# A chunked gated delta rule inside an eight-layer kernel: a feed-forward block is spread over another part of its work, and the second half's channels move beside the chunk recurrence

## The chip, the cores and the metric

The kernel runs on one core of a Trainium2 chip. The metric is device time in microseconds (us), from launch to end, as the median of several runs. One further execution was recorded by the hardware profiler, and all readings of single instructions come from it.

## The reference

The input is a batch of 1 x 1024 tokens of width 256. Eight blocks follow each other, each with a layer norm in front and a residual sum behind: `attn_a`, `ffn`, `attn_b`, `ffn` (the same weights as the first), `attn_c`, `moe`, `attn_d`, `moe`. The change touches the second to the fourth block only:

```python
# ffn: ternary weights, wq = clip(round(W / mean|W|), -1, 1) * mean|W|
hidden = silu(x @ wu.T) * (x @ wg.T)          # 256 -> 1024
y = hidden @ wd.T                             # 1024 -> 256

# attn_b: q, k (6 heads x 32) and v (6 heads x 64) pass a causal convolution of
# 4 taps and a silu, q and k are normalized, then token by token, per head:
S = S * exp(g_t)                              # S is 32 x 64
delta = (v_t - k_t @ S) * beta_t
S = S + outer(k_t, delta)
o_t = q_t @ S
# o is normalized per head, multiplied by silu(gate), and projected to 256
```

## The kernel before

The tokens are held as 8 tiles (chunks) of 128, in two halves of 512 (`HALF`). The function `middle` computes the second to the fourth block. The recurrence is not run token by token: within a chunk of 128 tokens it becomes matrix products with the inverse of a triangular matrix per head, and a state is carried from chunk to chunk.

Work is written as Python generators; each `yield` ends a step. `weave(main, side)` draws steps of `main` and, after each, on average `pace` steps of `side`; `at(rate, steps)` sets the pace while its steps are drawn. `one_by_one` runs generators after each other, `in_turn` alternates them, `staggered` starts one every few steps, and `times(3, ...)` yields only at every third step. The order in which steps are drawn is the order in which instructions are recorded; the framework then arranges each engine's instructions by its own estimate, and on the chip each engine runs its list strictly in order.

These generators matter:

- `ffn_steps(hf, ...)` (L597): the feed-forward block for one half. For each of 8 slices `e` of the 1024 hidden units it issues 6 bf16 matmuls for `f_wu` (tile `pf`), a silu on ScalarE, 6 bf16 matmuls for `f_wg`, a product on VectorE (`sl`), and `split`, which cuts the fp32 result into three bf16 pieces `hT` with ScalarE and GpSimd. Three slices later `second(e)` issues 12 matmuls into the two PSUM tiles `po`, which `sums()` takes. A last step adds `po` to the residual `x` (L647). There are 25 steps.
- `channels(hf, cv)` (L1131): the layer norm of a half (if not yet made), then for 6 groups `j` of 128 channels a projection (`pj`), a copy into `raw` (ScalarE), a convolution of one multiplication and three multiply-adds on VectorE (L797, L800), a silu, and transposes to tokens (`pt`, L817); for `q` and `k` also sums of squares (`pn`). In between come the projections for `g` and `beta` (`pg`).
- `products(hf, p)` (L1159): `decays` (`g`, and its exponentials through `pe`) and, per chunk, `prepare` (L849): GpSimd makes `kA`, `gm` and `qA`; TensorE multiplies `gm` and adds the causal mask (`pd`, L867 and L869), ScalarE takes the exponential, TensorE transposes (`pt`, L878) and multiplies (`pk`, L888), VectorE writes `am` (L892), and SyncE sends 4 pieces of it to DRAM (`dA`).
- `invert(hf, p)` (L903): one load of the 96 triangular blocks of 32 x 32 of a half (4 chunks), 31 elimination steps of two VectorE instructions each (L916, L922), and two stores. `relay` (L929) loads the results into `xi` and `xiT`.
- `turns(p)` (L1171): per chunk `complete` (first matmul `py`, L964), and the `chain` of the state, which runs one chunk behind. `leave` (L1067) normalizes a chunk's output, projects it (`pw`) and adds it to `x`.

The order in `middle` is written out by hand: the first half of the second block's feed-forward (L697); `channels(0)` with the second half of that feed-forward beside it at a pace of 0.75 (L1210); then one weave whose main line is `products(0)`, `invert(0)`, and then `relay`, `turns` and `leave` alternating, and whose side line is `second_half()` (L1229): `channels(1)` at 1.0, `products(1)` at 1.2, then `invert(1)` and `ahead`, which makes the fourth block's norm and the first half of its feed-forward once the first four chunks have left. The second half of that feed-forward comes last (L1248).

The PSUM pool of `middle` has five banks that all the small tiles share, and the two `po` tiles. The causal mask is added by a matmul of two fp32 operands, the mask and three copies of the identity:

```python
id3 = sq[:, IDENT : IDENT + 1, :].to_broadcast([P, GRP, P])
pe.matmul(pd, lhsT=sq[:, GT, :], rhs=gm[:, h0 : h0 + GRP, :], start=True, stop=False)
pe.matmul(pd, lhsT=sq[:, CAUSAL, :], rhs=id3, start=False, stop=True)
```

Of the kernel before, what the change touches and what calls it, by code (L numbers as in the profile page):

```python
# [15 lines left out]
BF16 = mybir.dt.bfloat16  # L16
# [6 lines left out]
P = 128  # L23
# [9 lines left out]
FF = 1024  # L33
# [4 lines left out]
IDENT, LE, GT, CAUSAL = range(4)  # L38
# [3 lines left out]
def hybrid_kernel(ctx: ExitStack, tc: tile.TileContext, w: dict, out: bass.AP):  # L42
# [554 lines left out]
    def ffn_steps(hf, wt, xT, p, bank, sums, beside=None):  # L597

        cols = slice(hf * HALF, (hf + 1) * HALF)
        po = sums()
        hT = {}

        def second(e):
            h = hT.pop(e)
            for t in range(HT):
                for n in range(3):
                    pe.matmul(  # L610
                        po[t // 2][:, t % 2, :],
                        lhsT=h[:, n, t * P : (t + 1) * P],
                        rhs=wt["f_wd"][:, e, :],
                        start=(e == 0 and t % 2 == 0 and n == 0),
                        stop=(e == FF // P - 1 and t % 2 == 1 and n == 2),
                    )

        for e in range(FF // P + 3):
            if e < FF // P:
                both = []  # L620
                for wn in ("f_wu", "f_wg"):
                    ps = bank("pf")
                    mm(
                        ps,
                        [
                            (wt[wn][:, k, e * P : (e + 1) * P], xT[:, n, k, cols])
                            for k in range(KC)
                            for n in range(3)
                        ],
                    )  # L630
                    if wn == "f_wu":
                        sl = p.tile([P, HALF], F32, tag="sl", name="sl")
                        act.activation(sl, ps, AF.Silu, scale=wt["f_sc"][:, 0, 0:1])  # L633
                        yield
                    else:
                        dve.tensor_tensor(sl, sl, ps, ALU.mult)  # L636
                hT[e] = p.tile([P, 3, HALF], BF16, tag="hT", name="hT", bufs=4)
                split(p, hT[e], sl, [HALF], pool)
                if beside:
                    beside()  # L640
                yield
            if e >= 3:
                second(e - 3)
                yield
        for t in range(HT):
            i = hf * HT + t
            dve.scalar_tensor_tensor(x[:, i, :], po[t // 2][:, t % 2, :], wt["f_both"], x[:, i, :], ALU.mult, ALU.add)  # L647
        yield


    def middle(wf, wt, n_f, norm, weights, following):
# [25 lines left out]
        with (  # L677
# [16 lines left out]

            f2 = right.enter_context(tc.tile_pool(name="f2", bufs=2, side="right", reuse_waits="tile"))
            n_f.need(0, bank)
            for _ in ffn_steps(0, wf, n_f.xT, f2, bank, sums, lambda: n_f.step(1, bank)):  # L697
                pass

            xT = norm.xT  # L700
            qk = b1.tile([P, NT, 2 * DH, DK], F32, tag="qk", name="qk")
# [13 lines left out]
            eT = b1.tile([ROWS, NT, 2], F32, tag="eT", name="eT")  # L715
            le6 = sq[:, LE : LE + 1, :].to_broadcast([P, DH, P])
            past = b1.tile([P, 6, 3], F32, tag="past", name="past")
            id3 = sq[:, IDENT : IDENT + 1, :].to_broadcast([P, GRP, P])

            def decays(hf, gb, p):  # L720

# [127 lines left out]
            def prepare(c, p):  # L849

                while c >= HOLD and c - HOLD not in done:
                    yield
                kA = two_of(pool, p, "kA", c, 0)
                gm = p.tile([P, DH, P], F32, tag="gm", name="gm")
                pool.tensor_tensor(gm, le6, g[:, c, :, None].to_broadcast([P, DH, P]), ALU.mult)
                qA = p.tile([P, 2, DH, DK], F32, tag="qA", name="qA")
                pool.tensor_tensor(
                    qA,
                    qk[:, c, None, :DH, :].to_broadcast([P, 2, DH, DK]),
                    cq[:, c, :, :, None].to_broadcast([P, 2, DH, DK]),  # L860
                    ALU.mult,
                )
                yield
                dT = p.tile([P, DH, P], F32, tag="dT", name="dT", bufs=2)
                for h0 in range(0, DH, GRP):
                    pd = bank("pd")[:, : GRP * P].rearrange("p (h n) -> p h n", h=GRP)
                    pe.matmul(pd, lhsT=sq[:, GT, :], rhs=gm[:, h0 : h0 + GRP, :], start=True, stop=False)  # L867

                    pe.matmul(pd, lhsT=sq[:, CAUSAL, :], rhs=id3, start=False, stop=True)  # L869
                    act.activation(dT[:, h0 : h0 + GRP, :], pd, AF.Exp)  # L870
                yield
                kqT = p.tile([ROWS, 2, 3, P], F32, tag="kqT", name="kqT")
                qGT[c] = hold.tile([ROWS, 2, P], F32, tag="qGT", name="qGT")
                for n in range(2):
                    hs = slice(n * GRP, (n + 1) * GRP)
                    pt = bank("pt")[:ROWS].rearrange("p (i n) -> p i n", i=4)
                    for i, src in enumerate((kA[:, 0, hs], kA[:, 1, hs], qA[:, 0, hs], qA[:, 1, hs])):
                        pe.transpose(pt[:, i, :], src.rearrange("p h d -> p (h d)"), ident)  # L878
                    act.copy(kqT[:, n], pt[:, :3, :])
                    act.copy(qGT[c][:, n], pt[:, 3, :])  # L880
                yield
                am[c] = hold.tile([P, DH, 2, P], F32, tag="am", name="am")
                for n in range(2):
                    made = []
                    for i in range(GRP):
                        r = slice(i * DK, (i + 1) * DK)
                        pk = bank("pk")[:, : 2 * P].rearrange("p (i n) -> p i n", i=2)
                        pe.matmul(pk, lhsT=kqT[r, n, 0, :], rhs=kqT[r, n, 1:, :], start=True, stop=True)  # L888
                        made.append(pk)
                    for i, pk in enumerate(made):  # L890
                        h = n * GRP + i
                        dve.tensor_tensor(  # L892
                            am[c][:, h], pk, dT[:, h : h + 1, :].to_broadcast([P, 2, P]), ALU.mult
                        )
                    yield
                for b in range(NB):
                    r = slice(b * BL, (b + 1) * BL)
                    nc.sync.dma_start(out=blocks(dA, c, b), in_=am[c][r, :, 0, r])
                yield
# [202 lines left out]
            def in_turn(*steps):  # L1102

                steps = list(steps)
                while steps:
                    steps = [s for s in steps if next(s, steps) is not steps]
                    yield

            def one_by_one(*steps):
                for s in steps:  # L1110
                    yield from s
# [47 lines left out]
            def products(hf, p):  # L1159

                yield from decays(hf, steps_of.pop(hf), p)
                lengths(hf, lens.pop(hf))
                cs = range(hf * HC, (hf + 1) * HC)
                for c in cs:
                    pool.tensor_tensor(
                        vb[:, c], vb[:, c], beta[:, c, :, None].to_broadcast([P, DH, DV]), ALU.mult
                    )
                yield
                yield from staggered(2, [prepare(c, p) for c in cs])
# [13 lines left out]
            def at(rate, steps):  # L1183

                pace[0] = rate
                yield from steps

            def weave(main, side):

                debt = 0.0  # L1190
                for _ in main:
                    debt += pace[0]
                    while debt >= 1.0:
                        next(side, None)
                        debt -= 1.0
# [11 lines left out]
            for pair in still:  # L1207
                for t in pair:
                    pool.memset(t, 0.0)
            side = at(0.75, ffn_steps(1, wf, n_f.xT, f2, bank, sums))  # L1210
            next(side)
            weave(channels(0, cv), side)
            for _ in side:
                pass
            right.close()
# [11 lines left out]
                yield from ffn_steps(0, wf, n_g.xT, f3[0], bank, sums)  # L1227

            def second_half():  # L1229
                yield from at(1.0, channels(1, cv))  # L1230
                yield from at(1.2, products(1, p2))
                fronts.close()
                yield from at(1.2, in_turn(one_by_one(times(3, invert(1, b3)), relay(1, 8)), ahead()))

            side = second_half()
            next(side)
            leaving = staggered(5, [leave(c, bt) for c in range(NT)])
            weave(
                one_by_one(
                    products(0, p2), times(3, invert(0, b3)), in_turn(relay(0, 6), turns(bt), leaving)  # L1240
                ),
                side,
            )
            for _ in in_turn(side, (n_g.step(1, bank) for _ in range(HT + 2))):
                pass
            right.close()
# [364 lines left out]
```

## Time and profile before

| | |
|---|---|
| time, median of 5 runs | 1779.19 us (1777.99 to 1783.81) |
| the profiled execution's own time | 1781.2 us |
| its span, first to last instruction | 1779.1 us |
| its mean granted TensorE clock | 0.940 |
| TensorE matmuls (PE) busy | 1612.2 us, 91% |
| VectorE (DVE) busy | 924.3 us, 52% |
| ScalarE (ACT) busy | 617.9 us, 35% |
| GpSimd (POOL) busy | 381.4 us, 21% |
| the part of `middle` that is rearranged | from 354.9 to 764.1 us of the span |

In the lines of the profile, PE is TensorE's matmuls, DVE VectorE, ACT ScalarE, POOL GpSimd and SP SyncE, which issues the DMAs. L12 is line 12 of the kernel. A line of the timeline gives the start, the time taken by one or several instructions that were merged, the instruction, and in brackets the idle time before it and what ended that. A table of windows gives for each stretch of the span the busy time of each engine, with the number of instructions, and the TensorE clock that was granted (1.00 is full speed). A full-rate matmul of 128 x 512 bf16 elements takes about 0.22 us when it follows another.

### The profile page before, as it was taken

The numbers are of one execution on the slowest core, as the hardware profiler recorded it, in microseconds if no ns is written. First come the engines' busy times: TensorE is split into PE (matmuls) and PEld (weight loads), VectorE is DVE, ScalarE is ACT, GpSimd is POOL, SyncE is SP. The second block draws the span as 40 slices with busy tenths as digits, with TensorE's granted clock in tenths as the row PEclk, the third lists the DMA queues.
The fourth block names the chain that finished last, engine by engine and source line by source line (L and its number), as shares of the span: only waits on it lengthen the run. The fifth ranks groups of instructions, "written<-read, shape, count | busy, mean of one in ns | idle before, by whom it ended". The sixth has DMA issues, their size and how long they took to land.

```text
span 1779.1 us, 23924 instructions
## 1 busy us (share of the span) xinstructions
PE 1612.2 (91%) x9655; PEld 747.6 (42%) x9674; DVE 924.3 (52%) x1762; ACT 617.9 (35%) x1117; POOL 381.4 (21%) x474
## 2 busy tenths in 40 slices
PE   7999999987749598789999998999889999998999
PEld 2433433544437366434333334454333333444454
DVE  7767675466736734357777634134554444533211
ACT  1466567445513131314554551111022222231100
POOL 2000002634213232440000000533101111230433
PEclk9999999997959698789999998999999999996999
DMA  5000000000010100120000001000000000000000
GB/s 185 1 1 1 1 2 1 1 1 0 18 34 19 25 10 1 45 99 1 1 1 1 2 1 55 1 1 0 0 1 1 1 1 1 1 1 1 1 12 12
DMA packets 33549, 24.23 MB, mean 14 GB/s; under 512 B 21888, under 2 KB 29776, under 8 KB 33440
## 3 DMA queue, kind: packets, MB, share of 16 engines
q1 hardware_dynamic: 32432, 18.89, 3.7%
q0 software_dynamic: 1008, 3.83, 0.6%
q8 instruction: 76, 1.25, 0.3%
q14 instruction: 33, 0.27, 0.0%
HBM read 19.10 MB, written 3.41 MB: 13 GB/s over the span
## 4 chain that ended last, share of the span: by engine, by line
PE 75%; DVE 15%; POOL 5%; issue 2%; ACT 2%; DMA 1%; SPq 0%; POOLq 0%; DVEq 0%; ACTq 0%
PE s L258 19%; PE st L258 9%; PE o L270 8%; PE po L160 5%; PE pj L160 4%; DVE mx L218 3%; PE py L1385 2%; PE pu L1370 2%; PE pu L1285 2%; PE pg L1285 2%; PE pg L1370 2%; PE pf L160 2%; PE stt L258 2%; POOL hT L101 1%; POOL rest L99 1%
## 5 line engine op out<-in xcount | busy, mean ns | idle before, releaser
L218 DVE TENSOR_REDUCE mx<-s 128x2 f32<-128x1024 f32 (+3 forms) x352 | 401.4, 1150 | 177.5 <-PE st L258 138.2
L258 PE MATMUL st<-qT,kT 32*128 32x512 f32 (+3 forms) x1288 | 390.1, 614 | 1.7 <-ACT pr L245 0.9
L258 PE MATMUL s<-kT,qT 32*128 32x512 f32 (+3 forms) x1408 | 358.0, 612 | 13.5 <-DVE mx L218 10.9
L243 ACT ACTIVATE pr<-st 128x512 f32<-128x512 f32 (+3 forms) x408 | 205.2, 553 | 266.7 <-PE st L258 211.1
L270 PE MATMUL o<-pr,V 128*32 128x256 f32 (+3 forms) x2240 | 200.2, 429 | 0.5
L245 ACT ACTIVATE pr<-st,bonus 128x512 f32<-128x512 f32 x236 | 149.5, 684 | 70.5 <-PE st L258 70.0
L258 PEld LDWEIGHTS s<-kT,qT 32*128 32x128 f32 x1408 | 102.6, 183 | 163.0 <-issue 133.1
L258 PEld LDWEIGHTS st<-qT,kT 32*128 32x128 f32 x1288 | 129.6, 183 | 17.6 <-ACT pr L243 6.5
L270 PEld LDWEIGHTS o<-pr,V 128*32 128x32 f32 x2240 | 45.4, 108 | 205.3 <-issue 188.2
L316 POOL TENSOR_TENSOR raw<-raw,rc 128x512 f32<-128x512 f32 x24 | 25.1, 1048 | 484.1 <-DVE rc L315 484.1
L1374 DVE TENSOR_TENSOR sl<-sl,pg 128x512 f32<-128x512 f32 (+1 forms) x48 | 32.9, 686 | 137.3 <-PE pg L1370 137.3
L258 PE MATMUL s<-kr,qr 64*128 64x512 f32 (+3 forms) x384 | 89.9, 542 | 11.0 <-DVE mx L218 7.6
L1375 POOL TENSOR_TENSOR hT<-sl,mask 128x512 f32<-128x512 f32 (+1 forms) x48 | 60.6, 1264 | 176.7 <-DVE sl L1374 176.7
L1372 ACT ACTIVATE sl<-pu 128x512 f32<-128x512 f32 (+1 forms) x48 | 28.6, 596 | 195.9 <-PE pu L1370 195.9
L258 PE MATMUL st<-qr,kr 64*128 64x512 f32 (+3 forms) x344 | 78.8, 501 | 0.0
L249 POOL TENSOR_SCALAR_AFFINE_SELECT pr<-pr 128x128 f32<-128x128 f32 x128 | 35.7, 294 | 181.0 <-ACT pr L243 179.7
L215 DVE TENSOR_TENSOR s<-s,squares 128x256 f32<-128x256 f32 x64 | 27.5, 429 | 78.2 <-PE s L258 73.6
L258 PEld LDWEIGHTS s<-kr,qr 64*128 64x128 f32 x384 | 30.3, 187 | 72.1 <-issue 21.3
L160 PE MATMUL pf<-xT,f_wu 128*128 128x512 bf16 x182 | 50.8, 403 | 3.3 <-ACT xT L100 1.6
L610 PE MATMUL po<-f_wd,hT 128*128 128x256 bf16 x384 | 48.4, 277 | 5.6 <-POOL hT L101 3.0
L1370 PE MATMUL pu<-z,m_up_B 128*128 128x512 f32 (+1 forms) x96 | 49.6, 599 | 0.0
L636 DVE TENSOR_TENSOR sl<-sl,pf 128x512 f32<-128x512 f32 x32 | 21.9, 686 | 53.1 <-ACT sl L633 30.0
(352 smaller groups left out, 2360.3 us busy)
## 6 DMA issues: line engine op xcount, KB each, us to landing
qT<-nmT SPq DMA_DIRECT2D x96, 2.0 KB
x<-in_x SPq DMA_DIRECT2D x8, 128.0 KB
raw_f_wu<-in_f_wu SPq DMA_DIRECT2D x1, 1024.0 KB
raw_f_wg<-in_f_wg SPq DMA_DIRECT2D x1, 1024.0 KB
raw_f_wd<-in_f_wd SPq DMA_DIRECT2D x1, 1024.0 KB
out<-x SPq DMA_DIRECT2D x8, 128.0 KB
b_wqkv<-in_b_wqkv SPq DMA_DIRECT2D x1, 768.0 KB
dA<-am SPq DMA_DIRECT2D x32, 24.0 KB
```

Of the source, the lines that this page charges most:

```text
L160: pe.matmul(ps, lhsT=a, rhs=b, start=(n == 0), stop=(n == len(pairs) - 1))
L218: dve.reduce_max(maxima[u][:, pair : pair + 2, t % HT, c // HALF], ps[:, :, :size], axis=AX.X, negate=True)
L243: act.activation(pr[:, js, :wide], ps, AF.Exp)
L245: act.activation(pr[:, js, :wide], ps, AF.Exp, bias=bias[:, kt : kt + 1])
L249: pool.affine_select(block, block, [[1, P]], ALU.is_ge, 0.0, base=0, channel_multiplier=-1)
L258: pe.matmul(dst, lhsT=a, rhs=b, start=(i == 0), stop=(i == len(parts) - 1))
L270: pe.matmul(sums[u][32 * j : 32 * j + 32, c0:c1], lhsT=V[:, kt, g * GH + j, :], rhs=weights[m][0][:, j, c0 - d : c1 - d], start=(kt == 0 a ...
L610: pe.matmul(po[t // 2][:, t % 2, :], lhsT=h[:, n, t * P : (t + 1) * P], rhs=wt["f_wd"][:, e, :], start=(e == 0 and t % 2 == 0 and n == 0), ...
L1285: pe.matmul(ps[:r], lhsT=wt[wn][:, k, es], rhs=xT[:, k, cols], start=(k == 0), stop=False)
L1370: pe.matmul(ps[:r], lhsT=wt[wn][:, es], rhs=z[hf, m, j], start=False, stop=True, skip_group_check=(j > 0))
L1375: pool.tensor_tensor(hT[:r], sl[:r], masks[3 + j][:r, cols], ALU.mult)
L1385: pe.matmul(ld[hf][j], lhsT=wt["m_down_A"][:r, e, :], rhs=tops_of[n, j][:r], start=(e == 0), stop=(e == HIDC - 1),)
```

## The change

Four edits, all in `middle` and in `ffn_steps`:

1. `sums()` is called when the first `second(e)` runs rather than at the start of the generator. The first half's feed-forward is run for 21 of its 25 steps only; its last four (three groups of 12 `po` matmuls, and the sum into `x`) are then drawn alternately with the first four steps of the second half's, and three more of these follow.
2. The rest of the second half's feed-forward is side work at a pace of 0.4 beside a main line of `channels(0)`, `products(0)`, `invert(0)` and `relay(0)`; what is left of it is drawn after that.
3. `channels(1)`, `products(1)`, `invert(1)` and `ahead` are side work beside `turns` and `leave` alone, at paces of 2.4 and, from `invert(1)` on, 1.0.
4. The identity and the causal mask are copied to bf16 tiles by GpSimd (two instructions in all), and the mask's matmul takes these.

```diff
-        po = sums()
-        hT = {}
+        po, hT = [], {}
         def second(e):
+            if e == 0:
+                po.extend(sums())
...
-            for _ in ffn_steps(0, wf, n_f.xT, f2, bank, sums, lambda: n_f.step(1, bank)):
-                pass
+            opening = ffn_steps(0, wf, n_f.xT, f2, bank, sums, lambda: n_f.step(1, bank))
+            for _ in range(2 * (FF // P) + 5):
+                next(opening)
...
-            id3 = sq[:, IDENT : IDENT + 1, :].to_broadcast([P, GRP, P])
+            ident16, causal16 = (b1.tile([P, P], BF16, tag=n, name=n) for n in ("ident16", "causal16"))
+            pool.tensor_copy(ident16, ident)
+            pool.tensor_copy(causal16, sq[:, CAUSAL, :])
+            id3 = ident16[:, None, :].to_broadcast([P, GRP, P])
...
-                    pe.matmul(pd, lhsT=sq[:, CAUSAL, :], rhs=id3, start=False, stop=True)
+                    pe.matmul(pd, lhsT=causal16, rhs=id3, start=False, stop=True)
...
-            side = at(0.75, ffn_steps(1, wf, n_f.xT, f2, bank, sums))
-            next(side)
-            weave(channels(0, cv), side)
+            side = at(0.4, ffn_steps(1, wf, n_f.xT, f2, bank, sums))
+            for _ in opening:
+                next(side)
+            for _ in range(3):
+                next(side)
+            weave(one_by_one(channels(0, cv), products(0, p2), times(3, invert(0, b3)), relay(0, 6)), side)
...
             def second_half():
-                yield from at(1.0, channels(1, cv))
-                yield from at(1.2, products(1, p2))
+                yield from at(2.4, channels(1, cv))
+                yield from products(1, p2)
                 fronts.close()
-                yield from at(1.2, in_turn(one_by_one(times(3, invert(1, b3)), relay(1, 8)), ahead()))
+                yield from at(1.0, in_turn(one_by_one(times(3, invert(1, b3)), relay(1, 8)), ahead()))
             side = second_half()
-            next(side)
             leaving = staggered(5, [leave(c, bt) for c in range(NT)])
-            weave(
-                one_by_one(
-                    products(0, p2), times(3, invert(0, b3)), in_turn(relay(0, 6), turns(bt), leaving)
-                ),
-                side,
-            )
+            weave(in_turn(turns(bt), leaving), side)
```

## The prediction

> **What bounds the kernel now.** I read the totals and slices of the page first, then busy time by windows over the rearranged part (354.9 to 764.1 us), then the PE timeline around its gaps.
>
> ```profile
> span 1779.1 us, 23924 instructions
> PE   7999999987749598789999998999889999998999
> PEclk9999999997959698789999998999999999996999
> ```
>
> PE is the limit nearly everywhere; the slices that fall to 4 and 5 lie in `middle`, and the clock falls with them. The windows show how much (columns: PE, PEld, DVE, ACT, POOL busy, granted clock):
>
> ```profile
> 369.00:413.00 44.00, 42.94 (x250) 27.32 (x252) 30.89 (x56) 26.20 (x45) 19.67 (x27) 1.00 0.00 1
> 413.00:421.20 8.20, 0.00 (x0) 0.00 (x0) 8.03 (x36) 3.58 (x5) 4.67 (x5) 0.72 0.00 0
> 431.30:463.40 32.10, 29.58 (x142) 17.02 (x140) 17.60 (x37) 19.80 (x38) 10.97 (x12) 0.89 0.06 10
> 480.10:509.60 29.50, 0.00 (x0) 0.03 (x1) 22.89 (x57) 2.86 (x4) 9.72 (x10) 0.58 0.10 29
> 509.60:528.40 18.80, 15.32 (x114) 12.20 (x115) 1.97 (x7) 3.90 (x9) 1.80 (x2) 0.50 0.22 34
> 528.40:568.20 39.80, 38.73 (x377) 28.59 (x375) 23.09 (x67) 15.61 (x37) 14.64 (x16) 0.99 0.05 9
> 594.00:623.60 29.60, 13.38 (x32) 6.42 (x33) 21.51 (x76) 6.39 (x12) 5.59 (x7) 0.62 0.17 39
> ```
>
> Where PE has a filler (369 to 413, 528 to 568) it is over 97% busy at full clock. It stands still for 8 us while the norm follows the feed-forward, for 29.5 us in the first inversion, and for half of 594 to 623.6 in the second. After a stop the clock stays at 0.50 for 18.8 us. The timeline names each stop's end:
>
> ```profile
> 360.60 0.69 PE L140 MATMUL u<-squares,xn 128*128 128x128 f32 x2 [4.38 <-DVE xn L137]
> 421.29 1.08 PE L140 MATMUL u<-squares,xn 128*128 128x128 f32 x4 [8.33 <-DVE xn L137]
> 431.36 0.81 PE L867 MATMUL pd<-gm,squares 128*128 128x384 f32 x2
> 432.01 0.81 PE L869 MATMUL pd<-squares 128*128 128x384 f32 x2
> 509.60 1.36 PE L964 MATMUL py<-xi,am 32*32 32x32 f32 x24 [29.59 <-DMA xi<-dX]
> 623.67 1.30 PE L964 MATMUL py<-xi,am 32*32 32x32 f32 x24
> ```
>
> Three moments carry the sum: first `pd` 431.4, first `py` 509.6 (turn 0), fifth `py` 623.7 (turn 4).
>
> **What the built order says.** In the changed kernel's PE list all 96 `pf` and 95 of the 96 `po` matmuls of the spread half stand before the first `pd`: at pace 0.4 beside some 34 channel steps, with seven drawn ahead, 20 of 25 steps are gone, and the framework puts the rest ahead of the products too. So nothing of the feed-forward fills inversion 0; PE only has two `pg` matmuls near its end. The work that did lie beside `products(0)`, `channels(1)`, is now among turns 0 to 3. `products(1)` ends inside turn 3 instead of before it. Before turn 4 the list has 48 `pf` and 20 `po` of the fourth block's feed-forward; in the trace 11 `pf` came before it. SP's DMAs keep their order. The two GpSimd copies (0.3 us each, half a 128x256 `rest` of 0.65) stand far ahead, where POOL idles; without that cover they cost 0.6. The later `sums()` costs nothing: `po` is free once L647 has read it, and its first matmul stands behind the norm's transposes.
>
> **Step 1, carried-over opening.** PE has five `pf` groups (1.3 us each: six matmuls 0.216 us apart) to do while DVE makes the norm, so the 4.38 us gap goes, and the half-clock rows behind it (2.77 and 2.13 us for six `pf` that take 1.46). PE work from 354.9 to 413: 9.04 + 42.94, less 2.6 for two groups done earlier, less 2 of half clock, plus 1 of waits = 48.4; it ends at 403. The gap of 8.3 goes too: the norm of half 1 no longer stands ahead of `products(0)`.
>
> **Step 2, to the first `pd`.** Behind the last `pf` (399.5) the chain is `sl` 0.69, cast 0.60, table load 1.28, Ln 0.22, nine small DVE operations 2.5, `gm` 1.47 and semaphores: 8 to 9 us. POOL has `rest`, `hT` and four `vb` (3.2) ahead of `gm` and is ready at about the same time. First `pd` at 408, 23 earlier; 4 us of PE wait are in it.
>
> **Step 3, `products(0)` alone.** Each chunk on PE: two `gm` matmuls 0.65, two masks, eight `pt` 0.87, six `pk` 1.28. The mask in fp32 shows two records and 0.65 us; in bf16 no row shows 384 columns, `pf` with 512 takes 0.216, so 0.16, bounded by 0.16 and 0.65. That is 0.48 x 16 = 7.7 us of PE over both halves, half on the path. 3.8 us per chunk plus waits on ACT and the five banks: 4.5 to 5, where the trace has 5.4 with PE full. Four chunks and a tail of 4.5: last `am` at 432 against 463.5.
>
> **Step 4, inversion 0.** From last `am` to first elimination 9.2 us (463.5 to 472.7), unchanged. The elimination took 31.8 with other DVE work between; alone it is twice its clean second half (492.47 to 504.43), 24.5. Then 5.2 to `py`. First `py` at 471 to 472: 38 earlier, though PE's gap grows from 29.5 to about 40.
>
> **Step 5, turns 0 to 3.** First `py` to last `pk` was 58 us. Added PE work: `pj` 6 x 1.72, `pt` 6 x 0.44, `pn` 3 x 0.82, `pg` 1.7, transposes 0.9, together 18; turn 3's first part 8; mask -4. At full clock the list from `py` to last `pk` sums to 72 us; 24 us at half clock at the start (18.8 in the trace, more gaps now) add 12. Then the waits. PE is in order, and the `pt` of a convolution stands ahead of turn matmuls: `pj`, copy 0.59, convolution 0.48 + 3 x 0.75, silu 0.63. On DVE the 14 small operations of `leave` (0.2 apart) now stand between multiply-adds. Following the lists by the rows I get stops of 1.2, 2.8, 2.8, 3.2 and 0.8 us in turns 1 to 3 and 6 at the start: 17. Sum 101, bounds 86 (72 + 12, and 2 of waits, by 528 to 568 with 1 us in 40) and 113 (the 17 and 12 both grown by 40%). Last `pk` at 573; it was 567.2. The 38 us are paid back.
>
> **Step 6, to turn 4.** Last `am` to elimination was 10.4 (DVE also has chunk 3's `vb` and `r` first): 584. It took 31.8 with `leave` between; now the fourth norm's `xn` and `rest` (4 x 0.8) and two `sl` are in its list, and the `sl` wait for `pf`: 35. Then 5.2, and PE ends its 20 `po` at about the same time: turn 4 at 626, against 623.7: +2.3.
>
> **Step 7, turns 4 to 7.** Feed-forward on PE behind that `py`: 85 x 0.216 + 96 x 0.109 = 28.8 us before, 48 x 0.216 + 76 x 0.109 = 18.7 now. Of the 10.1, 7.5 count: in turns 5 and 6 PE then meets the chain of `leave` (8.7 us from `po` at 649.8 to `pt` at 658.5). The rest to 764 is the same work.
>
> Sum: +2.3 - 7.5 = -5.2. The profiled execution took 1781.2 around its span of 1779.1; 1776.0 by its scale, 1774.0 by the median, which lies 2.0 lower.
>
> **A rule against the row.** The restart costs 9.4 us in the trace (18.8 at 0.50), and a gap of 2.5 us at 437 already brought 0.51 for 6 us. The Trainium skill, "TensorE: Matmul & The Clock Gate", section "What's actually happening", has the clock fall only after an idle window of about 3.4 us and return after as long a busy one. By an estimate from that page the restart would cost some 2 us, and the sum would be about -15. I keep the row. The same page, section "Why this matters for your kernels", warns of PE gaps above 3 us; this change removes two (4.4 and 8.3) and lengthens one.
>
> **Rivals.**
> *The chunk queue jams (slower).* DVE is in order; multiply-adds of 0.75 us, up to 1.7 where POOL reads too (L800 at 399.4), stand ahead of the evacuations `xi`, `xiT` and `state` of each turn. For: DVE would be 65% busy there, with PE waiting in order for both chains. Against: with DVE at 30.9 of 44 us in 369 to 413 PE still ran at 98%. From 107 us for step 5 the kernel is slower; at 113 it is +7: 1786; with inversion 1 stretched too, 1792.
> *The chunks hide the channels (much faster).* Waits as in 528 to 568: step 5 is 86, turn 4 15 earlier: 1759. Against: the half clock, and that inversion 1 still needs chunk 3's chain and the norm.
> *It does not do what it says.* No feed-forward in inversion 0 is already in the sum; the rival is that shifts cancel altogether, the mask's 4 us on the path being eaten by the longer gap: within 0.2% of 1779.
>
> **How the numbers follow.** 0.2% is 3.6 us, about what a measurement can tell. Faster 0.47: the forecast at 1774 (own range 1764 to 1775.6) with 0.33, the hidden channels with 0.14. Same 0.18. Slower 0.35: five in-order engine lists were followed by hand, and what such a walk leaves out only adds waits. The range takes 1758 to 1792: step 5 between 86 and 113, steps 1 to 4 within 4 us.
>
> **What would show it.** Right: no gap near 360; first `pd` near 408, first `py` near 471; PE empty for about 40 us before it; last `pk` near 573, turn 4 near 626; `pd` mask rows of one record, 0.16 to 0.25 us; fewer `pf` behind turn 4. Wrong: PE busy in the inversion; `py` after 480 (step 2 or 3 failed); `py` to last `pk` under 90 or over 110 us (step 5); turn 4 to the end of `middle` not shorter (step 7).

## The result and the profile after

The changed kernel takes 1774.5 us (median of 33 runs, 1772.1 to 1782.1), the kernel before, run beside it, 1780.9 us (median of 59). The ratio is 0.9969, 95% interval 0.9961 to 0.9976: 5.5 us faster (0.0031 x 1780.9). The forecast was 1774.0 and "faster" at 0.47. The profiled execution took 1773.3 us around a span of 1771.4.

From the page, PE's slices and its clock:

```profile
span 1771.4 us, 23888 instructions
PE   7999999997399698799999998999889999998999
PEclk9999999998587798789999998999999999996999
```

The low slices have changed places: where the feed-forward was carried over, the ninth slice rose from 8 to 9, and the dip of inversion 0 lies one slice earlier and is deeper (3, where it was 4). The PE timeline at the moments that the prediction named (start, length, instruction, idle time before it):

```profile
365.62 0.41 PE L140 MATMUL u<-squares,xn 128*128 128x128 f32 x2 [1.56 <-DVE xn L137]
408.58 0.59 PE L611 MATMUL po<-f_wd,hT 128*128 128x256 bf16 x3 [2.55 <-ACT hT L100]
412.74 1.49 PE L872 MATMUL pd<-gm,squares 128*128 128x384 f32 x2
414.02 0.53 PE L874 MATMUL pd<-ident,causal 128*128 128x384 bf16 x1
417.62 0.91 PE L872 MATMUL pd<-gm,squares 128*128 128x384 f32 x2
418.37 0.33 PE L874 MATMUL pd<-ident,causal 128*128 128x384 bf16 x1
418.54 0.81 PE L872 MATMUL pd<-gm,squares 128*128 128x384 f32 x2
471.87 0.82 PE L969 MATMUL py<-xi,am 32*32 32x32 f32 x12 [35.28 <-DMA xi<-dX]
580.88 1.12 PE L893 MATMUL pk<-kqT 32*128 32x256 f32 x6
630.15 0.53 PE L969 MATMUL py<-xi,am 32*32 32x32 f32 x12 [0.74 <-DMA xi<-dX]
761.64 2.98 PE L160 MATMUL pj<-xT,c_wq 128*128 128x512 f32 x4
```

The last line is the first matmul of the fifth block and marks the end of the rearranged part; before, it stood at 764.33. The first feed-forward matmul of `middle` came at 322.76 here and at 320.12 before, an offset of 2.64 that lies ahead of every edit, so moments are compared from that matmul on. So counted, the rearranged part took 444.2 us before and 438.9 after: 5.3 less, as the runs say. The spans differ by 7.7: by 2.7 up to that matmul (5.3 less 2.64), and by 5.0 behind it, where nothing was changed. That tail took 1009.6 to 1015.9 us in the thirteen traces of this case, whatever was edited ahead of it (1014.8 before, 1009.8 after), and its granted clock differs too (0.98 before and 1.00 after, from 1200 to 1350 us); it is no part of the gain.

### The profile page after: what moved, and what is told of

It is laid out like the page before. It is cut to its first block, busy times and chain, and to the rows that moved or that the text cites. A ratio compares the mean times of both kernels' runs of the same rounds, so it can differ in the third digit from the quotient of the medians.

```text
span 1771.4 us, 23888 instructions
## 1 busy us (share of the span) xinstructions
PE 1609.8 (91%) x9639; PEld 748.0 (42%) x9658; DVE 921.9 (52%) x1762; ACT 609.3 (34%) x1111; POOL 380.3 (21%) x476
## 3 DMA queue, kind: packets, MB, share of 16 engines
HBM read 19.10 MB, written 3.41 MB: 13 GB/s over the span
## 4 chain that ended last, share of the span: by engine, by line
PE 77%; DVE 15%; POOL 4%; issue 2%; ACT 1%; DMA 1%; SPq 0%; DVEq 0%; POOLq 0%; ACTq 0%
PE s L258 19%; PE st L258 9%; PE o L270 8%; PE po L160 5%; PE pj L160 4%; DVE mx L218 3%; PE pf L160 3%; PE pu L1287 2%; PE py L1387 2%; PE pu L1372 2%; PE pg L1287 2%; PE pg L1372 2%; PE stt L258 2%; PE po L611 1%; DVE X L927 1%
## 5 line engine op out<-in xcount | busy, mean ns | idle before, releaser
L245 ACT ACTIVATE pr<-st,bonus 128x512 f32<-128x512 f32 x236 | 149.5, 684 | 70.5 <-PE st L258 69.9
L611 PE MATMUL po<-f_wd,hT 128*128 128x256 bf16 x384 | 49.3, 278 | 6.6 <-ACT hT L100 4.1
L637 DVE TENSOR_TENSOR sl<-sl,pf 128x512 f32<-128x512 f32 x32 | 22.0, 686 | 56.8 <-ACT sl L634 33.4
```

The source lines that it names most:

```text
L245: act.activation(pr[:, js, :wide], ps, AF.Exp, bias=bias[:, kt : kt + 1])
L611: pe.matmul(po[t // 2][:, t % 2, :], lhsT=h[:, n, t * P : (t + 1) * P], rhs=wt["f_wd"][:, e, :], start=(e == 0 and t % 2 == 0 and n == 0), ...
```

## The experiments

Times are medians in us; the ratio is to runs of the kernel before in the same job. In the table the moments are us from the first feed-forward matmul of `middle`, from one profiled execution each. "py" is the first of turn 0, "turn 4" its first `py`, "end" the first matmul of the fifth block.

| kernel | time | ratio (95%) | first pd | first py | last pk ends | turn 4 | end |
|---|---|---|---|---|---|---|---|
| before | | 1 | 111.2 | 189.5 | 248.2 | 303.6 | 444.2 |
| changed | 1774.5 | 0.9969 (0.9961 to 0.9976) | 90.0 | 149.1 | 259.2 | 307.4 | 438.9 |
| e1 edit 4 alone | 1775.5 | 0.9981 (0.9970 to 0.9992) | 111.3 | 184.6 | 243.5 | 298.6 | 442.5 |
| e2 edit 1 alone | 1771.1 | 0.9954 (0.9937 to 0.9971) | 105.7 | 181.6 | 237.4 | 293.1 | 435.9 |
| e3 edits 1 and 4 | 1770.3 | 0.9944 (0.9929 to 0.9959) | 107.0 | 180.2 | 239.1 | 293.8 | 432.6 |
| e4 changed, feed-forward late | 1767.6 | 0.9928 (0.9913 to 0.9943) | 83.1 | 149.3 | 249.5 | 298.7 | 431.6 |
| e5 changed, channels slow | 1805.9 | 1.0143 (1.0119 to 1.0167) | 91.6 | 152.6 | 289.6 | 339.4 | 472.8 |
| e6 changed, channels fast | 1772.5 | 0.9955 (0.9941 to 0.9970) | 91.6 | 152.4 | 240.7 | 296.8 | 438.6 |
| e7 e4 and channels early | 1768.9 | 0.9937 (0.9924 to 0.9950) | 83.0 | 155.8 | 241.8 | 292.5 | 428.6 |
| e8 e7, faster | 1770.3 | 0.9936 (0.9923 to 0.9950) | 82.2 | 161.2 | 232.4 | 287.7 | 429.9 |
| e9 changed, PE kept busy | 1777.9 | 0.9993 (0.9970 to 1.0016) | 90.0 | 150.7 | 256.2 | 304.3 | 435.8 |
| e10 e4, PE kept busy | 1764.4 | 0.9914 (0.9896 to 0.9931) | 83.2 | 149.5 | 245.7 | 295.4 | 425.9 |
| e11 changed less edit 4 | 1781.2 | 1.0017 (0.9995 to 1.0038) | 90.0 | 155.5 | 264.0 | 312.1 | 443.7 |

### One part at a time: e1, e2, e3, e11

**e1** is the kernel before with edit 4 alone:

```diff
-                    pe.matmul(pd, lhsT=sq[:, CAUSAL, :], rhs=id3, start=False, stop=True)
+                    pe.matmul(pd, lhsT=causal16, rhs=id3, start=False, stop=True)
```

> The kernel before with edit 4 alone (mask and identity in bf16). Theory A (the prediction's terms): a mask matmul falls from 0.65 to about 0.17 us, 16 x 0.48 = 7.7 us of TensorE, half of it on the path, because products(0) and products(1) run with TensorE 92 to 97% busy in the kernel before: 3.5 to 8 us faster than before, first py 3 to 4 us earlier, fifth py 4 to 7 earlier. Rival B (the mask is hidden; products are paced by ScalarE's exponential and the five shared banks, and the re-weaving alone earned the result): within 1.5 us of before, first py not moved by over 1 us. Rival C (the mask is the whole result and the re-weaving nets nothing): 4.3 to 7 us faster, as the whole change was.

3.4 us faster (0.0019 x 1780; 1.4 to 5.3 by the interval): just under theory A's 3.5 to 8, with an interval that reaches into its range and into rival C's, while rival B (within 1.5) is all but out. The first `py` came 4.9 earlier, turn 4 5.0 earlier, and the end 1.7. At full clock the rows give what was worked out. In the kernel before:

```profile
448.24 0.91 PE L867 MATMUL pd<-gm,squares 128*128 128x384 f32 x2
448.99 0.81 PE L869 MATMUL pd<-squares 128*128 128x384 f32 x2
449.63 0.81 PE L867 MATMUL pd<-gm,squares 128*128 128x384 f32 x2
```

A `gm` matmul and its mask took 1.39 us there (448.24 to 449.63) and 0.92 in the changed kernel (417.62 to 418.54, above): 0.47 less for each mask. The Trainium skill, "FP8 and Floating Point Precision", section "TensorE Precision Notes", gives a true fp32 product four passes through the array; the rows agree, with 0.64 us for the fp32 mask and 0.16 to 0.17 from a bf16 mask to the next matmul.

**e2** is the kernel before with edit 1 alone:

```diff
-            for _ in ffn_steps(0, wf, n_f.xT, f2, bank, sums, lambda: n_f.step(1, bank)):
-                pass
+            opening = ffn_steps(0, wf, n_f.xT, f2, bank, sums, lambda: n_f.step(1, bank))
+            for _ in range(2 * (FF // P) + 5):
+                next(opening)
...
-            next(side)
+            for _ in opening:
+                next(side)
+            for _ in range(3):
+                next(side)
```

> The kernel before with edit 1 alone: the first half's feed-forward ends beside the start of the second's, everything behind it is woven as before. Theory A: the gap of 4.38 us near 360 and the half clock behind it go, some 7 us of TensorE time; the gap of 8.3 us before products(0) stays, since the second norm still stands ahead. First pd 6 to 8 us earlier than 431.4, and as nothing behind it is changed, the time falls by 5 to 8 us. Rival B: the channels' DVE chain sets the first pd, not TensorE: first pd moves by under 2 us, time within 2 us of before. If A holds, the re-weaving behind the opening (edits 2 and 3) must have cost about what the opening gave.

8.2 us faster: theory A, at the upper end of its 5 to 8, though the first `pd` is only 5.6 earlier (6 to 8 expected). The end is 8.3 earlier. **e3** adds edit 4 to it:

> The kernel before with edits 1 and 4: the opening and the mask, without the re-weaving of products, inversion and channels. Theory A: the two gains add, 9 to 14 us faster than before, so 4 to 8 us faster than the whole change; the re-weaving (edits 2 and 3) is then a loss of that size. Rival B: the gains do not add, because what comes earlier waits at the inversion or at turn 4: 4 to 7 us faster than before, the same as the whole change, and the re-weaving is worth nothing either way. Rival C: the re-weaving earns the result: under 4 us faster than before.

10.0 us faster, theory A's additive case within the intervals (8.2 and 3.4). It is also faster than the whole change, whose interval (0.9961 to 0.9976) lies above e3's: edits 2 and 3, the re-weaving, cost 4.5 us (0.0025 x 1780), 6.3 by the traces. The table shows where. With them the first `pd` is 17 us earlier and the first `py` 31 earlier, but the last `pk` 20 later and turn 4 13.6 later; the turns behind it win 7.4 back. **e11** takes edit 4 out of the changed kernel:

> The changed kernel without edit 4: the mask's matmul stays in fp32. Theory A (step 3 of the prediction: 7.7 us of TensorE, half of it on the path): products(0) longer by 2 to 4 us, first py 2 to 4 us later, products(1) likewise, together 2 to 6 us slower than the changed kernel, so about as fast as the kernel before. Rival B (products(0) alone is paced by the chain over ScalarE's exponential, VectorE's am and the five banks, and products(1) by the turns around it): first py within 1 us, time within 1.5 us of the changed kernel; the whole gain is then the weaving's.

8.5 us slower than the changed kernel by the ratios (0.0048 x 1779; 6.7 by the medians), and not faster than the kernel before. That is above theory A's 2 to 6, but the two intervals together (some 4.5 to 12.6 us) reach into it. So edits 1 to 3 together brought nothing that shows, and taken away last the mask is worth the whole result; put in alone (e1) it was worth 3.4, so what an edit is worth depends on the others. The trace puts 6.3 us into `products(0)` alone (first `pd` to the end of the last `pk` 30.2 us, 23.8 in the changed kernel), and nothing into the part from first `py` to last `pk` (108.5 and 110.1). This split, of one execution each, is partly the clock's: it was lower in e11's `products(0)` (0.82, against 0.87 in the changed kernel) and higher in its turns (0.80 against 0.76). Each length times (1 - clock) gives 2.3 us more lost in the first and 4.3 less in the second; eight masks by the rows are 3.8 us in each. PE has little to spare in `products(0)` alone (idle for 2.6 of 23.8 us), and part of it runs at half clock, where the fp32 mask rows, 0.64 apart at full clock, are 1.28 apart:

```profile
431.12 1.49 PE L871 MATMUL pd<-squares 128*128 128x384 f32 x2
432.40 1.49 PE L869 MATMUL pd<-gm,squares 128*128 128x384 f32 x2
```

### What sets turn 4, and what turn 4 is worth: e5, e6

```diff
-                yield from at(2.4, channels(1, cv))
+                yield from at(1.2, channels(1, cv))      # e5
+                yield from at(5.0, channels(1, cv))      # e6
```

> The changed kernel with the second half's channels drawn at 1.2 instead of 2.4 beside the turns, so that products(1) comes behind more of the turns. Theory A (the chain channels(1), products(1), inversion 1 sets turn 4, and turn 4 sets the end): last pk and turn 4 come 8 to 20 us later; of that 4 to 14 us stay at the end: slower than the changed kernel by 4 to 14 us. Theory B (turns 0 to 3 are bound by the sum of TensorE's work and its half clock, whatever the order, and what turn 4 loses the turns behind it win): within 3 us of the changed kernel.

31 us slower than the changed kernel (1.0143 - 0.9969), more than twice theory A's bound. The last `pk` is 30 later, turn 4 32, the end 34: all of a delay of `channels(1)` and `products(1)` goes to the end.

> The changed kernel with the second half's channels drawn at 5.0 instead of 2.4, so that they and products(1) stand in turns 0 and 1 and turns 2 and 3 beside inversion 1. Theory A (the chain sets turn 4): last pk 25 to 40 us earlier, turn 4 5 to 15 us earlier, 4 to 12 us faster than the changed kernel. Theory B (only the sum of work and half clock counts): within 3 us of it. Rival C (slower): turns 2 and 3 beside the elimination stretch it, since VectorE is in order, and turns 0 to 3 no longer cover products(1): turn 4 not earlier, 2 to 8 us slower.

2.5 us faster than the changed kernel by the ratios, intervals overlapping: theory B's size, not A's, though turn 4 came 10.6 earlier, as A had it (last `pk` 18.5, for A's 25 to 40). The end moved 0.3. Two windows of e6, last `pk` to turn 4 and turn 4 to the last `pw` (columns as before: PE, PEld, DVE, ACT, POOL, clock):

```profile
561.20:617.30 56.10, 37.14 (x236) 27.58 (x235) 39.20 (x130) 9.16 (x16) 8.62 (x9) 0.73 0.09 25
617.30:713.60 96.30, 85.16 (x765) 61.11 (x764) 37.54 (x112) 28.59 (x58) 32.96 (x32) 0.91 0.05 8
```

The same stretches of the changed kernel:

```profile
582.00:630.10 48.10, 29.21 (x121) 16.72 (x121) 36.99 (x113) 13.88 (x24) 13.51 (x14) 0.75 0.11 29
630.10:715.00 84.90, 72.50 (x686) 54.53 (x692) 32.43 (x102) 19.67 (x41) 23.55 (x23) 0.89 0.05 9
```

In e6 turn 3 and the rest of turn 2 fill inversion 1, and the fourth block's feed-forward, which waits for chunk 3 to leave, follows turn 4 instead of preceding it (no `pf` matmul stands ahead of turn 4, 47 in the changed kernel): 12.7 us more of PE stands there (85.16 against 72.50). Turn 4 earlier is worth nothing when the work that filled the inversion is pushed behind it; turn 4 later is paid in full.

### Filling inversion 0: e4, e7, e8

```diff
-            side = at(0.4, ffn_steps(1, wf, n_f.xT, f2, bank, sums))
+            side = at(0.1, ffn_steps(1, wf, n_f.xT, f2, bank, sums))
...
+            def faster(rate):
+                pace[0] = rate
+                yield
-            weave(one_by_one(channels(0, cv), products(0, p2), times(3, invert(0, b3)), relay(0, 6)), side)
+            weave(
+                one_by_one(channels(0, cv), products(0, p2), faster(1.2), times(3, invert(0, b3)), relay(0, 6)), side
+            )
```

> The changed kernel with the spread feed-forward at a pace of 0.1 beside channels(0) and products(0) and 1.2 from inversion 0 on, so that 36 pf and 45 po matmuls (8 and 5 us of TensorE) stand between the last pk and the first py. Theory A (what the prediction missed nothing of: the inversion of 35 us leaves TensorE empty, and work put there is free and is gone from the part ahead of products): first pd 8 to 12 us earlier, first py 6 to 11 us earlier at about 462 to 466, less half clock behind it: 6 to 13 us faster than the changed kernel. Rival B: VectorE is in order, and the products sl (0.69 us each) and the sum into x now stand between the elimination's instructions, and the norm of the second half and channels(1) come later by as much: first py at 468 to 474, time within 3 us of the changed kernel. Rival C (slower): the norm of the second half moves behind the inversion and turns 0 to 3 grow by more than is won: 3 to 10 us slower than the changed kernel.

12.8 us below the kernel before, 7.3 below the changed one: theory A's time, but B's mechanism at the inversion. The first `pd` came 6.9 earlier and the last `pk` of `products(0)` 7.8, and the first `py` not at all (149.1 and 149.3): the elimination grew by what was won. Its DVE timeline:

```profile
434.16 1.14 DVE L927 TENSOR_TENSOR X<-X,by 96x31 f32<-96x31 f32 x1
435.20 0.68 DVE L637 TENSOR_TENSOR sl<-sl,pf 128x512 f32<-128x512 f32 x1
437.27 1.11 DVE L921 TENSOR_TENSOR by<-X,A 96x112 f32<-96x112 f32 x1
438.41 1.11 DVE L927 TENSOR_TENSOR X<-X,by 96x112 f32<-96x112 f32 x1
```

and its GpSimd timeline at the same time:

```profile
437.07 1.17 POOL L101 TENSOR_TENSOR hT<-rest,hT 128x512 bf16<-128x512 f32 x1 [0.73 <-ACT hT L100]
438.21 1.18 POOL L99 TENSOR_TENSOR rest<-sl,hT 128x512 f32<-128x512 f32 x1
```

In the changed kernel the instructions of 96 x 112 take 0.27 us; here they take 1.11 and end within 0.2 us of GpSimd's. What shortened the end is first `py` to last `pk`: 100.2 us for 110.1. PE was idle for 9.6 us of it here and 7.6 in the changed kernel (the windows below), so stops do not explain it; the lost clock, reckoned as below, fell from 26.6 to 17.7 us (470.1 to 570.3 in e4). Some 30 matmuls of turn 3 (3.3 us by the changed kernel's rows) also stand behind the last `pk` in e4, so the clock is not the whole of the 9.9. **e7** keeps e4 and also begins `channels(1)` in inversion 0, **e8** begins it faster and draws the rest at 5.0:

```diff
-            side = at(0.1, ffn_steps(1, wf, n_f.xT, f2, bank, sums))
+            rest, ch = ffn_steps(1, wf, n_f.xT, f2, bank, sums), channels(1, cv)
+            side = kept = one_by_one(at(0.1, rest), ch)     # e8: and faster(2.0)
...
-                yield from at(2.4, channels(1, cv))
+                yield from at(2.4, ch)                      # e8: at(5.0, ch)
```

> The kernel of e4 (spread feed-forward partly in inversion 0) with the second half's norm and first projections drawn from inversion 0 on, at 1.2, behind that feed-forward. Theory A (the empty 27 us of TensorE in inversion 0 are free for channels, and turn 4 hangs on channels(1)): first py up to 3 us later, turn 4 3 to 10 us earlier than in e4, 3 to 9 us faster than e4, about 1760. Rival B (inversion 0 is bound by VectorE, and each instruction put between the elimination's goes on its length): first py 3 to 8 us later, turn 4 within 3 us of e4, time within 3 us of e4.

> As e7 with a pace of 2.0 from inversion 0 on and 5.0 beside the turns: all of channels(1) stands before the first py, products(1) in turns 0 to 2. Theory A: first py 8 to 15 us later than in e4 (the convolutions, 6 x 2.7 us of VectorE, lie between the elimination's instructions), last pk 20 to 40 us earlier, turn 4 8 to 20 us earlier, 6 to 15 us faster than e4. Rival B: VectorE's elimination takes the whole of it, turns 2 and 3 stretch inversion 1 as well, turn 4 not earlier: 0 to 8 us slower than e4.

Both stay within the interval of e4 (by the ratios 1.6 and 1.4 us slower). The first `py` comes 6.5 and 11.9 us later, turn 4 comes 6 and 11 us earlier, as theory A had it, and the end only 3.0 and 1.7: rival B in time, with the same exchange as in e6 (ahead of turn 4 stand 42 `pf` matmuls in e4, 18 in e7, none in e8).

### Is it the half clock: e9, e10

```diff
+            def warm(n):
+                ps = bank("pf")
+                for _ in range(n):
+                    pe.matmul(ps, lhsT=wf["f_wu"][:, 0, :P], rhs=n_f.xT[:, 0, 0, :HALF], start=True, stop=True)
+                yield
-            weave(one_by_one(channels(0, cv), products(0, p2), times(3, invert(0, b3)), relay(0, 6)), side)
+            weave(one_by_one(channels(0, cv), products(0, p2), warm(156), times(3, invert(0, b3)), relay(0, 6)), side)
```

> The changed kernel with 156 added bf16 matmuls of 128x512, whose result nothing reads (33.7 us at 0.216), between the last pk of products(0) and the first py, so that TensorE is busy through inversion 0 and ends about 1.5 us before the first py. Theory A (the half clock behind a stop is what made step 5 long: 471.8 to 494 us ran at 0.50 and 0.63, 9.5 us of lost clock): first py unmoved, granted clock 0.9 to 1.0 behind it, first py to last pk 6 to 10 us shorter, time 4 to 10 us faster than the changed kernel. Rival B (turn 0 is bound by the loads of xi and xiT and by the chain to ScalarE and back, so the clock is not on the path): clock full, but first py to last pk shorter by under 3 us, time within 2 us. Rival C (the clock is lost to how much TensorE runs, not to stops): half clock appears elsewhere, in turns 0 to 3 or before, time same or slower.

> The kernel of e4 with 122 such added matmuls (26.4 us) behind the last po, up to about 1 us before the first py. Theory A: 470 to 492 us ran at 0.50 and 0.79 in e4, 7.5 us of lost clock: first py unmoved, time 3 to 8 us faster than e4, 1760 to 1765, the fastest of all. Rival B: within 2 us of e4. Rival C: slower than e4.

e10 puts `warm(122)` behind e4's first weave. The two windows behind the first `py`, of e10:

```profile
470.30:480.00 9.70, 9.37 (x99) 6.33 (x100) 3.09 (x8) 2.33 (x6) 1.00 (x1) 0.82 0.33 49
480.00:492.00 12.00, 12.00 (x103) 7.66 (x102) 8.98 (x15) 6.27 (x12) 1.89 (x3) 1.00 0.09 15
```

and of e9:

```profile
475.30:486.00 10.70, 9.68 (x102) 7.57 (x102) 2.67 (x7) 1.96 (x5) 0.99 (x1) 0.69 0.31 48
486.00:496.00 10.00, 9.54 (x39) 4.94 (x39) 3.69 (x5) 2.32 (x5) 1.08 (x1) 0.64 0.09 13
```

In e10 a gap of 1.22 us was left before `py` (27.53 in e4), the clock behind it was 0.82 and then full (0.50 and 0.79 in e4), first `py` to last `pk` shrank by 3.9 us, and the end by 5.7. By the ratios it is 2.5 us below e4, between theory A (3 to 8) and rival B (within 2), of which the intervals (0.9896 to 0.9931, 0.9913 to 0.9943) leave the sign open; it is the fastest kernel here, 0.9914 of the kernel before. In e9 a gap of 2.07 us was left, and the clock stayed at 0.69 and 0.64. Its profiled execution still won 4.6 us from first `py` to last `pk`, but its 12 runs spread from 1766 to 1790 us and their median is not below the changed kernel's: theory A was not met. The runs' times follow their own granted clock (0.952 at 1766, 0.938 at 1790); where in the runs that were slower the clock was lost is open.

## Why the prediction was right or wrong

The sum (-5.2) met the trace (-5.3) and the runs (-5.5), with steps that were off in both directions. In the list, the first number is measured and the one behind "for" is forecast; moments are from the first feed-forward matmul of `middle` (the forecast's less 320.12).

1. **Opening: right.** The 4.38 gap is 1.56, the `pf` groups at 357.42 to 364.06 run 1.3 us apart at full clock, the gap of 8.3 is gone. e2 shows that edit 1 alone is worth 8 us, though there a gap before the products stays (4.55 us).
2. **First `pd`:** 90.0 for 87.9, 2 late. 2.55 us of PE's wait is the last `hT` piece, and behind it the first chunk ran at half clock.
3. **`products(0)` alone: the length was right, the term of the mask mis-sized.** 24.8 us from the first `pd` to the last `am`, for 24. But the mask was counted with 3.9 us here and 4 in the turns; e11 shows 6.3 and nothing, its clock included, and 4.5 to 12.6 us by the runs.
4. **Inversion 0: 34.4 us from last `am` to first `py`, for 38.9.** The elimination began 6.2 after the last `am`, not 9.2, and took 23.1, not 24.5 (twice 492.47 to 504.43 is 23.9, and that counts the middle step twice). The gap on PE was 35.3, forecast 40. No feed-forward stood in it, as foretold.
5. **Turns 0 to 3: the step that was most off, 109 us for 101,** inside its bounds (113), just under the 110 named as a sign of failure (110.1 to the end of the last `pk`), and past the 107 from which the queue rival was to be slower. The two terms were both mis-sized. The changed kernel's windows from the first `py` to the last `pk`:

```profile
471.80:482.00 10.20, 9.57 (x86) 6.83 (x87) 1.05 (x3) 2.87 (x5) 0.99 (x1) 0.50 0.31 47
482.00:494.00 12.00, 11.54 (x40) 7.19 (x39) 4.28 (x8) 2.30 (x5) 1.00 (x1) 0.63 0.10 16
494.00:505.00 11.00, 10.60 (x121) 7.90 (x121) 8.88 (x18) 5.85 (x11) 2.22 (x4) 1.00 0.00 0
505.00:515.40 10.40, 8.24 (x61) 6.47 (x59) 6.58 (x21) 3.59 (x7) 1.36 (x3) 0.97 0.01 2
515.40:521.50 6.10, 6.10 (x35) 4.59 (x35) 3.26 (x9) 0.62 (x2) 0.00 (x0) 0.50 0.00 0
521.50:528.00 6.50, 6.50 (x73) 5.13 (x73) 5.80 (x16) 2.28 (x5) 1.83 (x2) 1.00 0.01 3
528.00:543.00 15.00, 14.36 (x100) 12.68 (x97) 7.78 (x31) 7.20 (x12) 4.77 (x6) 0.54 0.01 2
543.00:551.00 8.00, 6.39 (x60) 5.05 (x61) 3.50 (x16) 5.75 (x11) 3.89 (x4) 0.86 0.00 0
551.00:561.50 10.50, 10.37 (x56) 6.73 (x54) 4.61 (x12) 3.13 (x8) 5.61 (x6) 0.78 0.00 0
561.50:570.00 8.50, 6.89 (x37) 4.34 (x37) 6.20 (x21) 2.02 (x6) 4.04 (x4) 0.76 0.08 14
570.00:582.00 12.00, 12.00 (x85) 7.36 (x83) 4.74 (x14) 4.84 (x14) 3.09 (x3) 0.89 0.09 15
```

   PE is idle for 7.6 us of these 110.2 (110.2 - 102.6), where 17 of waits had been walked through; each length times (1 - clock) adds to 26.6 us, an upper bound since it counts PE's stops too, where 12 had been put for half clock. The rest, some 76 us, is the work put at 72. VectorE's queue hardly stops PE; the clock does. At the start it was half for 18.9 us (471.9 to 490.8), less than the 24 counted; the other 17 us of the loss lie from 515 us on, where the sum had none.
6. **To turn 4: 49.3 us from last `pk`, for 53.** The elimination began 8.7 after the last `am` and took 33.4, for 10.4 and 35. Turn 4 is 3.8 later than before (2.3 forecast).
7. **Turns 4 to 7: -9.2 us to the end, for -7.5.** More of the 10.1 counted.

**The rivals.** The queue rival had its mark (over 107) but neither its cause nor its sign: the first `py` 2.3 us early, and 3.7 and 1.7 us won in steps 6 and 7, made up for it. The hidden channels fell with step 5. "The shifts cancel" was nearest to what lay behind: of the changed kernel's parts, the opening won 8, the re-weaving lost 4.5 (with the mask in 16 bits) to 11 (without, e11 against e2), and what the mask saves is left. The sum did not price the edits apart and missed step 5 by 8 us, so that it came within half a us is luck; that the changed kernel would be slightly faster, with the moments near those named, was foreseen.

**The rule against the row.** Keeping the row was right, and the clock cost still more than the row had it: by the page's window the sum was -15, and the runs gave -5.5. Even gaps of 1.2 and 2.1 us, below the idle window of 3.4 that the Trainium skill, "TensorE: Matmul & The Clock Gate", section "What's actually happening", states, were followed by a clock of 0.82 and 0.69 here (e10, e9). The advice of its section "Why this matters for your kernels", to leave no PE gaps above 3 us, was worth 5.7 us of trace at inversion 0 in e10.

## What to carry over

When a rearrangement moves several parts at once, run each part alone: here the two cheap edits (a late sum that lets matmuls stand beside a norm, a mask in 16 bits) gave more than the whole, and the large one took part of it away again. A half with a long latency chain (channels, products, inversion) should start early; delaying it by 30 us cost all of them, and pulling it 10 us forward won nothing, since the filler of its inversion moved behind it. A stop of a few us should be priced with the half clock that follows it, and so should a stretch of small matmuls (see below); a filler for VectorE's elimination should bring no work for VectorE or GpSimd.

## What the hardware showed that had not been expected

The clock halved without a new stop. Behind a wait of 1.86 us that ended at 513.38, the timeline of the changed kernel lists no gap on PE until 534.9; the granted clock in that stretch:

```profile
511.26:514.67 3.41, 1.55 (x14) 1.29 (x13) 1.16 (x5) 1.67 (x4) 0.99 (x1) 1.00 0.00 0
514.67:521.50 6.83, 6.83 (x39) 5.30 (x39) 3.68 (x10) 0.62 (x2) 0.00 (x0) 0.50 0.00 0
521.50:524.91 3.41, 3.41 (x45) 2.10 (x44) 2.78 (x10) 2.08 (x4) 1.00 (x1) 1.00 0.00 0
524.91:528.33 3.42, 3.42 (x38) 3.31 (x34) 3.03 (x7) 0.20 (x1) 0.83 (x1) 1.00 0.02 5
528.33:541.98 13.65, 13.01 (x69) 11.58 (x67) 7.60 (x30) 6.47 (x10) 3.75 (x4) 0.50 0.00 1
```

It was half, then full, then half again, with PE 100% busy from 514.67 to 534.9. The stretches are whole steps of 3.41 us: in all thirteen traces the clock is 0.50 or 1.00 for such a step at a time. What goes with it is not how long PE is busy but how much of its array is at work. To reckon that, count for each matmul record the columns streamed, times the share of the 128 x 128 array that its tile takes, an fp32 record as two passes (two records of 384 columns take 0.64 us, one in bf16 0.16), and divide by what a step holds at 512 columns in 0.216 us. The step from 511.26 comes to 0.27 and the one from 524.91, with matmuls of 64 x 64 tiles, 12 columns and the like, to 0.24, and the clock of the next step is half both times; the steps from 507.85 and 521.50 come to 0.64 and 0.71, and the next clock is full. Of the 1658 steps from 330 to 765 us in the thirteen traces, 478 come to less than 0.31, and all but one are followed by half clock; 1045 come to 0.38 or more, and all are followed by full clock; in between it is either. PE's busy share tells them apart far less well: behind 973 steps in which it was at least 95% busy, the clock was half 90 times. No run was made to test this, and some matmul records may be missing from a trace. Behind inversion 0, where the clock stayed half until 490.8, turn 0's small matmuls came to 0.06 to 0.28 a step up to 487.4, and the next step, with full-size projections, to 0.47.

VectorE's small instructions took 1.11 us instead of 0.27 while GpSimd wrote a 128 x 512 tile, and ended just behind it (e4). Seven of the elimination's instructions from 434 to 443 us took 4.9 us more than the same ones in the changed kernel, the greater part of the 8 by which the elimination grew. The Trainium skill, "GPSIMD Engine Reference", section "1. Specifications", says that GpSimd shares its SBUF interfaces with VectorE and that they contend when a VectorE instruction has two inputs in SBUF, as these have; the trace agrees. `sl` at 435.20, with one input in PSUM, took its usual 0.68 us beside a GpSimd instruction that ran from 435.19 to 436.35.
